# Second convolution over four neighbouring columns at a time, on column tiles of TensorE

## The chip, the cores and the metric

The kernel runs on one core of a Trainium2 chip. The metric is the device time of one execution in microseconds (us). Everything is fp32.

## The reference

The input x has 32 images of 96 channels and 56 x 56 points. Two layers follow each other:

```python
# layer 0
h = depthwise_conv7x7(x) + conv_b                 # per channel
h = layernorm over channels, * ln_g + ln_b
h = gelu(h @ w1 + b1) @ w2 + b2                   # 96 -> 384 -> 96 channels
x = h * layer_scale + x
# layer 1
xs = silu(depthwise_conv5x5(x) + conv_b)          # the "second convolution"
dts, Bs, Cs = split(x_proj_w @ xs)                # 6 + 4 + 4 rows for each point
delta = softplus(dt_w @ dts + dt_b)
log_dA = maximum(delta * A, log(1e-9))            # A < 0, 4 states for each channel
P = exp(cumsum(log_dA)); hs = P * cumsum(delta * Bs * xs / maximum(P, 1e-9))
y = sum over states (hs * Cs) + xs * Ds           # cumsums over the 3136 points
```

## The kernel before

The kernel runs four stages, one behind the other; each hands its result to the next through a buffer in DRAM (`conv1_d`, `block_d`, `conv2_d`), because the axis on partitions changes.

1. *First convolution* (lines 235 to 300). A loop over the 96 channels. Image rows stand on partitions, and a 7x7 depthwise convolution becomes products of TensorE with a banded (Toeplitz) matrix of weights. ScalarE adds the bias (L278), POOL stores to `conv1_d` (L282). Copies of the input into its padded layout are made by POOL (L265), DVE (L262) and ScalarE (L263, L266). The statistics of the layer norm are summed beside it on DVE.
2. *MLP* (lines 306 to 412). A loop over 28 groups of four rows, each for both halves (`s`: even and odd columns) of 448 points. `hidden` multiplies with w1 (L351, row tiles of TensorE), ScalarE applies gelu (L361), `result` multiplies with w2 (L370: four products of 32 output rows each, at four column tiles, one for each of the four image rows). DVE then adds bias and residual (L382), and POOL stores the group's rows of 32 channels to `block_d` (L391), one DMA for each group and block of channels. `normalise` (L341) scales the next group's input on DVE. The order of TensorE and DVE is written out by hand (`pin`): in each step the three parts `hidden`, `result`, `normalise` follow each other for f = 0, 1, 2. Accumulator `po` has two buffers.
3. *Second convolution* (lines 414 to 446). A loop over 96 channels. A tile `xp` holds a channel's 56 rows twice: the even columns on partitions 0 to 55, the odd ones from 64. For each channel three products (taps t = 1, 0, 2) are made for each half of the images (`j`), each with 120 input rows, 128 output rows (56 for even columns, 56 for odd ones, 16 unused) and 432 or 448 points (L429). Two ScalarE passes of 56 rows apply bias and silu and interleave even and odd columns (L441), and POOL stores 56 rows of 7168 bytes to `conv2_d` (L446). SP loads the weights (two DMAs by `toeplitz`, L226) and the two halves of the input (L423) for each channel; `wts` and `xps` have three buffers each, so loads run up to three channels ahead. PSUM has four accumulators.
4. *Scan* (from line 448). A loop over units of 32 channels and 1568 points, with DVE scans (L582, L591), POOL products (L575, L602) and ScalarE exponentials. It reads `conv2_d`.

The tap tables `taps1_d` and `taps2_d` in DRAM are made from the weights in a preparation part at the start (lines 140 to 158), where L153 copies single elements of the 5x5 weights in reversed order.

Of the kernel before, what the change touches and what calls it, by code (L numbers as in the profile page):

```python
# [23 lines left out]
WP = 128  # L24
W2 = W // 2
MP = 64
P1, P2 = (K1 + 1) // 2, (K2 + 1) // 2
CH = 1568
NI = 2
NCH = L // CH  # L30
# [11 lines left out]
def convnext_then_scan_kernel(  # L42
# [25 lines left out]

    conv1_d = dram.tile([C, ROWS, COLS], F32, name="conv1_d")
    block_d = dram.tile([C, ROWS, COLS], F32, name="block_d")
    conv2_d = dram.tile([C, H, B * W], F32, name="conv2_d")
    du_d = dram.tile([B * NCH, C, 2, CH], F32, name="du_d")
    rstd_d = dram.tile([ROWS, COLS], F32, name="rstd_d")
    taps1_d = dram.tile([C, 3 * WP * P1], F32, name="taps1_d")
    taps2_d = dram.tile([C, 3 * WP * P2], F32, name="taps2_d")

    def column(src, n, name):
        t = const.tile([n, 1], F32, name=name)  # L80
# [54 lines left out]
    with tc.tile_pool(name="prep", bufs=1) as prep, tc.tile_pool(  # L135
        name="prep_ps", bufs=1, space=PSUM
    ) as prep_ps:


        for taps_d, cw, k, flip in ((taps1_d, c1w, K1, False), (taps2_d, c2w, K2, True)):  # L140
            kt = prep.tile([C, k, k], F32, name=f"kt{k}")
            nc.sync.dma_start(kt, cw.rearrange("c (i j) -> c i j", j=k))
            pad = prep.tile([C, 3, WP, (k + 1) // 2], F32, name=f"pad{k}")
            nc.vector.memset(pad, 0.0)
            at = H - 1 - k // 2
            for i in range(3):
                for t in range((k + 1) // 2):
                    j = 2 * t + 1 - i
                    if j not in range(k):
                        continue  # L150
                    if flip:
                        for r in range(k):
                            nc.vector.tensor_copy(  # L153
                                pad[:, i, at + r, t : t + 1], kt[:, k - 1 - r, j : j + 1]
                            )
                    else:
                        nc.vector.tensor_copy(pad[:, i, at : at + k, t], kt[:, :, j])
            nc.sync.dma_start(taps_d, pad.rearrange("c d p t -> c (d p t)"))


        cen = prep.tile([C, C], F32, name="cen")
        nc.vector.tensor_scalar(cen, ident[:C, :C], -1.0 / C, None, ALU.add)
        w1g = prep.tile([C, F], F32, name="w1g")
        nc.vector.tensor_scalar(w1g, w1_t, g_t, None, ALU.mult)
        ps = prep_ps.tile([C, 512], F32, name="ps_w1")
        nc.tensor.matmul(ps[:, :F], lhsT=cen, rhs=w1g, start=True, stop=True)
        for i in range(RB):
            for d in range(C // CB):
                nc.vector.tensor_copy(
                    w1r_t[CB * i : CB * i + CB, d, :], ps[CB * d : CB * d + CB, :F]  # L170
                )
        ps = prep_ps.tile([128, 512], F32, name="ps_b1")
        for f in range(3):
            nc.tensor.matmul(
                ps[:, f : f + 1], lhsT=w1_t[:, f * 128 : (f + 1) * 128], rhs=lnb_t,
                start=True, stop=True,
            )
        nc.vector.tensor_add(b1p_t, ps[:, :3], b1_t)

        for f in range(3):  # L180
            nc.vector.tensor_mul(w2_t[:, f, :], w2_t[:, f, :], ls_b)
        b2p_t = prep.tile([C, 1], F32, name="b2p_t")
        nc.vector.tensor_mul(b2p_t, b2_t, ls_t)
        for i in range(RB):
            for d in range(C // CB):
                nc.vector.tensor_copy(
                    b2r_t[CB * i : CB * i + CB, d : d + 1], b2p_t[CB * d : CB * d + CB]
                )

        ps = prep_ps.tile([C, 512], F32, name="ps_wd")  # L190
        nc.tensor.matmul(ps[:, :C], lhsT=xp_t, rhs=dtwT_t, start=True, stop=True)
        nc.vector.tensor_copy(wd_t, ps[:, :C])


        nc.vector.memset(bcw_t, 0.0)
        nc.vector.tensor_copy(bcw_t[:, : 2 * N], xpT_t[:, R:])
        nc.vector.memset(pick_t, 0.0)
        for k in range(4):
            rows = slice(32 * k, 32 * k + 2 * N)
            at = 32 * k + (k // 2) * N  # L200
            nc.vector.tensor_copy(
                pick_t[rows].rearrange("p (d n) -> p d n", n=N),
                ident[rows, at : at + N].rearrange("p (o n) -> p o n", o=1).to_broadcast(
                    [2 * N, DG, N]
                ),
            )
        nc.vector.tensor_reduce(
            sel_t, ident.rearrange("p (d n) -> p d n", n=N), mybir.AxisListType.X, ALU.add
        )
        nc.vector.tensor_scalar(dsm_t, ident[:C, :C], ds_t, None, ALU.mult)  # L210
        nc.scalar.activation(a_t, a_t, AF.Exp)
        nc.vector.tensor_scalar(a_t, a_t, -1.0, None, ALU.mult)
# [19 lines left out]
    def two(t):  # L232
        return t.rearrange("p (s q) -> p s q", s=2)
# [72 lines left out]
    with tc.tile_pool(name="mlp", bufs=2) as pool, tc.tile_pool(  # L306
# [5 lines left out]
        hts: dict = {}  # L312
        xts: dict = {}
        gts: dict = {}
        ots: dict = {}

        def rows_of(d, row, b):
            return d[CB * b : CB * b + CB, row : row + RB, :].rearrange("c r q -> r c q")
# [47 lines left out]
        def result(n, s, d):  # L366
            po = ps_o.tile([128, 512], F32, name=f"po_{n}_{s}_{d}", tag="po")
            for f in range(3):
                for i in range(RB):
                    pin(nc.tensor.matmul(  # L370
                        po[CB * i : CB * i + CB, :HALF],
                        lhsT=w2_t[:, f, CB * d : CB * d + CB],
                        rhs=gts[n, s, f, i // 2][:, i % 2],
                        start=(f == 0),
                        stop=(f == 2),
                        tile_position=(0, CB * i),
                    ))
            if s == 0:
                ots[n, d] = pool.tile([128, COLS], F32, name=f"o_{n}_{d}", tag="o", bufs=5)
            ot = ots[n, d]  # L380
            pairs = "p (i r) -> p i r"
            pin(nc.vector.scalar_tensor_tensor(  # L382
                two(ot)[:, s].rearrange(pairs, i=BI),
                in0=po[:, :HALF].rearrange(pairs, i=BI),
                scalar=b2r_t[:, d : d + 1],
                in1=xts[n, d].rearrange("p (i r s) -> p s i r", i=BI, s=2)[:, s],
                op0=ALU.add,
                op1=ALU.add,
            ))
            if s == 1:  # L390
                nc.gpsimd.dma_start(rows_of(block_d, n * RB, d), ot)  # L391

        groups = ROWS // RB
        parts = groups * 2
# [14 lines left out]
                    normalise(n + 1, f)  # L409


    with tc.tile_pool(name="c2", bufs=3) as pool, tc.tile_pool(
        name="c2k", bufs=1
    ) as keep, tc.tile_pool(name="c2_ps", bufs=4, space=PSUM) as psum:
        wts = [keep.tile([128, 2, MP * P2], F32, name=f"wt2_{i}") for i in range(3)]
        xps = [keep.tile([128, B2, PQ], F32, name=f"xp2_{i}") for i in range(3)]
        for t in wts + xps:
            nc.vector.memset(t, 0.0)
        for c in range(C):
            wv = toeplitz(taps2_d, wts[c % 3], K2, c, MP)  # L420
            xt = xps[c % 3]
            for s in range(2):
                nc.sync.dma_start(xt[MP * s : MP * s + H], by_row(block_d[c], s))  # L423
            ps = psum.tile([128, B2, 512], F32, name=f"ps2_{c}", tag="ps")

            for i, t in enumerate((1, 0, 2)):
                lo, hi = max(0, 1 - t), W2 - max(0, t - 1)
                for j in range(B2):
                    nc.tensor.matmul(  # L429
                        ps[:, j, :PQ].rearrange("p (i r) -> p i r", i=BI)[:, :, lo:hi],  # L430
                        lhsT=wv[:KR, t],
                        rhs=xt[:KR, j].rearrange("p (i r) -> p i r", i=BI)[
                            :, :, lo + t - 1 : hi + t - 1
                        ],
                        start=(i == 0),
                        stop=(i == 2),
                    )
            st = pool.tile([H, B2, BI, W2, 2], F32, name=f"st_{c}", tag="st")
            for s in range(2):
                rows = slice(MP * s, MP * s + H)  # L440
                nc.scalar.activation(  # L441
                    st.rearrange("p j i r s -> p s j i r")[:, s],
                    ps[rows, :, :PQ].rearrange("p j (i r) -> p j i r", i=BI),
                    AF.Silu, bias=c2b_t[rows, c : c + 1], scale=1.0,
                )
            nc.gpsimd.dma_start(conv2_d[c], st.rearrange("p j i r s -> p (j i r s)"))  # L446

# [272 lines left out]
```

## Time and profile before

| | us |
|---|---|
| median of three runs | 3753.94 (3751.75 to 3754.26) |
| the profiled execution | 3750.96 |
| its span, first to last instruction | 3749.2 |
| first convolution, products (L270) | 27 to 608 |
| MLP, products (L351, L370) | 644 to 1487 |
| second convolution, products (L429) | 1506 to 1931 |
| scan | 1945 to the end |

| engine | busy us | share of the span |
|---|---|---|
| TensorE products (PE) | 3181.4 | 85% |
| weight loads (PEld) | 1445.6 | 39% |
| VectorE (DVE) | 2270.6 | 61% |
| ScalarE (ACT) | 2276.7 | 61% |
| GpSimd (POOL) | 1877.6 | 50% |

The profile is of one execution. A line such as L429 is a line of the kernel. A group of instructions is given with its engine, operation, output and input names, the shape (partitions x elements), the count, and behind the bar its busy time, the mean length in ns, and the idle time of the engine ahead of it with what ended that. A window line gives start and end of a stage, its length, the busy time of PE, PEld, DVE, ACT and POOL with their counts, the granted TensorE clock, the DMA share and GB/s. Lengths of matmul records are modelled and overlap, so a mean length times a count is not their busy time.

### The profile page before, as it was taken

What the parts mean: (1) busy time and instruction counts of PE and PEld (TensorE: products, weight loads), DVE (VectorE), ACT (ScalarE), POOL (GpSimd) and SP (SyncE); (2) the same over time, 40 slices, a digit from 0 to 9 for tenths busy, and PEclk for the clock granted to TensorE, in tenths of its full rate; (3) what the DMA queues carried; (4) which work ended last, traced back from release to release, by engine and by line L of the source; (5) the groups of instructions that cost most, each with busy time, mean ns of one, the idle gap of its engine ahead of it and who ended that gap; (6) DMA issues with size and microseconds to landing.
All of it is one profiled execution on the core that took longest, in us unless ns stands there. A gap on an engine that the chain in (4) does not pass through costs nothing. (4 is left out here: it accounts for less than half of the span.)

```text
span 3749.2 us, 41885 instructions
## 1 busy us (share of the span) xinstructions
PE 3181.4 (85%) x15370; PEld 1445.6 (39%) x15370; DVE 2270.6 (61%) x1413; ACT 2276.7 (61%) x2133; POOL 1877.6 (50%) x1085
## 2 busy tenths in 40 slices
PE   7999995999999998999976777877787777777775
PEld 5777773333333333666641222222222222222221
DVE  5666664222222222000008999999999999999998
ACT  3555552433333333444438888788878888888884
POOL 2333331000000000011117889889988988998896
PEclk9999997999999999999986666666767666676766
DMA  5555553455544553777768787778778777777873
GB/s 150 167 168 166 169 165 103 143 160 160 161 157 154 155 157 101 207 220 221 224 178 286 262 272 258 254 278 273 257 260 274 250 261 280 268 259 262 276 253 114
DMA packets 318352, 785.65 MB, mean 210 GB/s; under 512 B 137028, under 2 KB 201860, under 8 KB 293572
## 3 DMA queue, kind: packets, MB, share of 16 engines
q1 hardware_dynamic: 260996, 628.66, 52.2%
q0 software_dynamic: 42816, 115.77, 9.9%
q10 hardware_dynamic: 14336, 38.54, 2.7%
q8 instruction: 122, 2.00, 0.2%
q14 instruction: 82, 0.67, 0.1%
HBM read 550.06 MB, written 232.64 MB: 209 GB/s over the span
## 5 line engine op out<-in xcount | busy, mean ns | idle before, releaser
L602 POOL TENSOR_TENSOR hs<-hs,ct 128x1568 f32<-128x1568 f32 x192 | 672.9, 3505 | 104.1 <-DVE hs L591 89.4
L575 POOL TENSOR_TENSOR rep<-rep,bt 128x1568 f32<-128x1568 f32 x192 | 674.6, 3514 | 14.7 <-DMA rep<-du_d 14.7
L361 ACT ACTIVATE g<-ph,b1p_t 128x896 f32<-128x896 f32 x336 | 320.2, 1004 | 500.7 <-PE ph L351 500.7
L270 PE MATMUL ps<-xq,wt 120*112 120x448 f32 x1536 | 581.8, 540 | 13.0 <-POOL xq L265 13.0
L382 DVE SCALAR_TENSOR_TENSOR o<-po,b2r_t,x 128x448 f32<-128x448 f32 x168 | 114.8, 684 | 636.4 <-PE po L370 620.7
L270 PEld LDWEIGHTS ps<-xq,wt 120*112 120x112 f32 x1536 | 429.4, 280 | 165.0 <-POOL xq L265 13.3
L351 PE MATMUL ph<-h,w1r_t 32*128 32x448 f32 x4032 | 441.2, 561 | 47.8 <-DVE h L341 44.0
L391 POOL DMA_DIRECT2D block_d<-o x84 | 57.9, 689 | 820.2 <-DVE o L382 735.1
L429 PE MATMUL ps<-xp,wt 120*128 120x432 f32 (+1 forms) x1152 | 425.2, 533 | 17.8 <-DMA xp<-block_d 17.8
L506 PE MATMUL pz<-xs,wd_t 96*96 96x392 f32 x512 | 273.5, 699 | 174.1 <-ACT du L514 145.4
L370 PE MATMUL po<-g,w_t 128*32 128x448 f32 x4032 | 413.0, 543 | 0.0
L615 PE MATMUL py<-hs,sel_t 128*32 128x392 f32 x1536 | 332.9, 685 | 79.4 <-POOL hs L602 79.2
L582 DVE TENSOR_TENSOR_SCAN pv<-rep,pv 128x1568 f32<-128x1568 f32 x96 | 329.1, 3428 | 58.3 <-DMA rep<-du_d 41.8
L551 PE MATMUL pk<-bn,pick_t 8*128 8x392 f32 x1024 | 287.1, 678 | 90.5 <-ACT y L625 70.6
L587 DVE SCALAR_TENSOR_TENSOR pv<-pv,rep 128x1568 f32<-128x1568 f32 x192 | 345.6, 1800 | 20.0
L429 PEld LDWEIGHTS ps<-xp,wt 120*128 120x128 f32 x1152 | 289.7, 252 | 153.5 <-issue 21.3
L582 DVE TENSOR_TENSOR_SCAN pv<-rep,carry_p,pv 128x1568 f32<-128x1568 f32 x96 | 334.9, 3489 | 10.0 <-DVE hs L591 0.4
L591 DVE TENSOR_TENSOR_SCAN hs<-rep,carry_h,pv 128x1568 f32<-128x1568 f32 x96 | 334.0, 3480 | 11.1 <-DVE pv L587 1.4
L441 ACT ACTIVATE st<-ps,c2b_t 56x896 f32<-56x896 f32 x192 | 204.4, 1065 | 214.8 <-issue 210.3
L591 DVE TENSOR_TENSOR_SCAN hs<-rep,pv 128x1568 f32<-128x1568 f32 x96 | 328.3, 3420 | 9.9 <-DVE pv L587 0.5
L608 PE MATMUL py<-xs,dsm_t 96*96 96x392 f32 x512 | 314.6, 758 | 13.2 <-ACT bn L539 8.0
L569 ACT ACTIVATE rep<-rep,a_t 128x1568 f32<-128x1568 f32 x192 | 308.3, 1606 | 11.6 <-DMA rep<-du_d 11.3
(84 smaller groups left out, 3335.2 us busy)
## 6 DMA issues: line engine op xcount, KB each, us to landing
rep<-du_d SPq DMA_DIRECT2D x192, 1568.0 KB
du_d<-du SPq DMA_DIRECT2D x128, 588.0 KB
xt<-in_x_dram SPq DMA_DIRECT2D x192, 196.0 KB
h<-conv_d SPq DMA_DIRECT2D x84, 448.0 KB
x<-in_x_dram SPq DMA_DIRECT2D x336, 112.0 KB
block_d<-o POOLq DMA_DIRECT2D x84, 448.0 KB, 11.0
xp<-block_d SPq DMA_DIRECT2D x192, 196.0 KB
conv_d<-st POOLq DMA_DIRECT2D x96, 392.0 KB, 4.5
```

The lines of the kernel that those rows point to most:

```text
L270: nc.tensor.matmul(ps[:, j, :PQ].rearrange("p (i r) -> p i r", i=BI), lhsT=wv[:KR, t], rhs=xq[:KR, j, :, t : t + W2], start=(t == 0), stop ...
L351: pin(nc.tensor.matmul(phs[i // 2][:, i % 2, :HALF], lhsT=w1r_t[rows, d, f * 128 : (f + 1) * 128], rhs=hts[n, d][rows, s * HALF : (s + 1) ...
L361: nc.scalar.activation(gt, ph[:, :, :HALF], AF.Gelu, bias=b1p_t[:, f : f + 1], scale=1.0)
L370: pin(nc.tensor.matmul(po[CB * i : CB * i + CB, :HALF], lhsT=w2_t[:, f, CB * d : CB * d + CB], rhs=gts[n, s, f, i // 2][:, i % 2], start=( ...
L429: nc.tensor.matmul(ps[:, j, :PQ].rearrange("p (i r) -> p i r", i=BI)[:, :, lo:hi], lhsT=wv[:KR, t], rhs=xt[:KR, j].rearrange("p (i r) -> p ...
L575: pin(nc.gpsimd.tensor_mul(ut, ut, bts[i // NG]))
L582: pin(nc.vector.tensor_tensor_scan(run, da, zero, carry_p[:, col : col + 1] if q else 1.0 / EPS, ALU.mult, ALU.add))
L587: pin(nc.vector.scalar_tensor_tensor(run, in0=run, scalar=1.0, in1=ut, op0=ALU.min, op1=ALU.mult))
L591: pin(nc.vector.tensor_tensor_scan(ht, da, run, carry_h[:, col : col + 1] if q else 0.0, ALU.mult, ALU.add))
L602: pin(nc.gpsimd.tensor_mul(ht, ht, cts[k]))
L608: pin(nc.tensor.matmul(half(py[:C], s), lhsT=dsm_t, rhs=tokens(k, 2 * h + s, 4), start=True, stop=False,))
L615: pin(nc.tensor.matmul(py[g * DG : (g + 1) * DG, s, :BK], lhsT=sel_t, rhs=hss[k * NG + g][:, cols], start=False, stop=True, tile_position= ...
```

## The change

The second convolution is laid out anew, and with it what writes its input.

- `block_d` holds, for each channel and row, four sets of 14 columns (`k`), each set with one zero column as padding, in the order in which the second convolution reads it. The two DVE operations of a pair of halves become four, one for each of the four column sets, of 224 elements instead of 448; a group's store becomes four DMAs, one for each image row. Six output buffers are kept and zeroed once.
- The second convolution gives half of the rows (28 of 56) at a time. An input tile holds 30 rows times four column sets, 120 partitions; the tile has 128, and those that aren't loaded stay zero. For each half, two taps and four column sets of the output: eight products of 128 input rows, 32 output rows (28 used) and 448 points, each at its own column tile of TensorE.
- One ScalarE pass over 128 partitions takes the place of two over 56. Its result `yt` has the four column sets on four blocks of 32 partitions, so four copies of 28 rows (one on POOL, three on DVE) interleave the columns into `st`, which POOL stores.
- The weights of a channel come in one DMA of 128 rows of 1 KB from a new tap table.

```diff
-    block_d = dram.tile([C, ROWS, COLS], F32, name="block_d")
+    block_d = dram.tile([C, H, QC, B2, BI * QP], F32, name="block_d")
...
+        turned = prep.tile([C, K2, K2], F32, name="turned")
+        for r in range(K2):
+            nc.vector.tensor_copy(turned[:, r], kt[:, K2 - 1 - r])
+        pad = prep.tile([C, QC, 2 * RW, QC * 2], F32, name="pad2")
+        nc.vector.memset(pad, 0.0)
+        for k in range(QC):
+            for f in range(QC):
+                for t in range(2):
+                    j = 4 * t + (k if k < 2 else k - 4) - f + K2 // 2
+                    if j in range(K2):
+                        nc.vector.tensor_copy(
+                            pad[:, k, RW - K2 : RW, f * 2 + t], turned[:, :, j]
+                        )
+        nc.sync.dma_start(taps2_d, pad)
...
-        ots: dict = {}
+        ots = [
+            pool.tile([128, QC, BI, QP], F32, name=f"o_{i}", bufs=1) for i in range(2 * blocks)
+        ]
+        for t in ots:
+            nc.vector.memset(t, 0.0)
...
-            pin(nc.vector.scalar_tensor_tensor(
-                two(ot)[:, s].rearrange(pairs, i=BI),
-                in0=po[:, :HALF].rearrange(pairs, i=BI),
...
+            for e in range(2):
+                pin(nc.vector.scalar_tensor_tensor(
+                    ot[:, 2 * e + s, :, e : e + QW],
+                    in0=po[:, :HALF].rearrange("p (i a e) -> p e i a", i=BI, e=2)[:, e],
+                    scalar=b2r_t[:, d : d + 1],
+                    in1=xts[n, d].rearrange("p (i a e s) -> p s e i a", i=BI, s=2, e=2)[:, s, e],
...
-                nc.gpsimd.dma_start(rows_of(block_d, n * RB, d), ot)
+                for i in range(RB):
+                    nc.gpsimd.dma_start(
+                        rows[:, i], ot[CB * i : CB * i + CB].rearrange("p k i r -> p k (i r)")
+                    )
...
+            wt = pool.tile([128, RW * QC * 2], F32, name=f"wt2_{c}", tag="wt")
+            taps = taps2_d[c, 0, 0:1, 0:1]
+            step = QC * 2
+            nc.sync.dma_start(
+                wt,
+                bass.AP(
+                    taps.tensor, taps.offset,
+                    [[step, RW], [2 * RW * step, QC], [1, RW * step]],
+                ),
+            )
+            wv = wt.rearrange("p (o f t) -> p f t o", f=QC, t=2)
...
+            for h in range(2):
+                xt = xqs[c % 3][h]
+                rows = block_d[c, (H - RW + 2) * (1 - h) : (H - RW + 2) * (1 - h) + RW - 2]
+                nc.sync.dma_start(
+                    xt[2 * QC * h : 2 * QC * h + (RW - 2) * QC],
+                    rows.rearrange("m k j q -> (m k) (j q)"),
+                )
+                xv = xt.rearrange("p (b r) -> p b r", r=QP)
+                for t in range(2):
+                    for f in range(QC):
+                        nc.tensor.matmul(
+                            ps[RW * f : RW * f + RW, h, : B * QW].rearrange(
+                                "p (b q) -> p b q", q=QW
+                            ),
+                            lhsT=wv[:, f, t],
+                            rhs=xv[:, :, t : t + QW],
+                            start=(t == 0),
+                            stop=(t == 1),
+                            tile_position=(0, RW * f),
+                        )
+            yt = pool.tile([128, 2, B * QW], F32, name=f"yt_{c}", tag="yt")
+            nc.scalar.activation(
+                yt, ps[:, :, : B * QW], AF.Silu, bias=c2b_t[:, c : c + 1], scale=1.0
+            )
+            st = pool.tile([QR, 2, B, QW, QC], F32, name=f"st_{c}", tag="st")
+            for f in range(QC):
+                copy = nc.gpsimd.tensor_copy if f == 0 else nc.vector.tensor_copy
+                copy(
+                    st[:, :, :, :, f],
+                    yt[RW * f : RW * f + QR].rearrange("p h (b q) -> p h b q", q=QW),
+                )
+            nc.gpsimd.dma_start(
+                conv2_d[c].rearrange("(h o) w -> o h w", h=2),
+                st.rearrange("p h b q f -> p h (b q f)"),
+            )
```

## The prediction

> **What bounds the kernel now.** I read the page's slices first, then busy time by stage, then the second convolution's rows, and last the order of time at one group boundary of the MLP.
>
> The stages, with busy time and count of PE, PEld, DVE, ACT and POOL, then granted clock, DMA share and GB/s:
>
> ```profile
> 674.00:1490.00 816.00, 811.29 (x7944) 296.30 (x7940) 195.67 (x249) 312.47 (x328) 57.90 (x84) 1.00 0.48 151
> 1490.00:1506.00 16.00, 0.43 (x1) 0.46 (x2) 3.55 (x6) 0.00 (x0) 0.00 (x0) 0.59 0.50 141
> 1506.00:1930.00 424.00, 424.00 (x1151) 289.08 (x1151) 0.00 (x0) 203.63 (x191) 48.77 (x95) 1.00 0.75 217
> ```
>
> The second convolution (third row) is a TensorE stage: busy for all of its 424 us at full clock, DVE at nothing, POOL issuing DMAs only. But DMA is already at 0.75 there: the second limit stands a quarter away. In the MLP DMA and POOL have room.
>
> Rows by form (busy us, mean ns):
>
> ```profile
> L429 PE MATMUL ps<-xp,wt 120*128 120x432 f32 x768 | 294.7, 527 | 0.0
> L370 PE MATMUL po<-g,w_t 128*32 128x448 f32 x4032 | 413.0, 543 | 0.0
> L441 ACT ACTIVATE st<-ps,c2b_t 56x896 f32<-56x896 f32 x192 | 204.4, 1065 | 214.8 <-issue 210.3 <-PE ps L429 3.2
> L361 ACT ACTIVATE g<-ph,b1p_t 128x896 f32<-128x896 f32 x336 | 320.2, 1004 | 500.7 <-PE ph L351 500.7
> L262 DVE COPY xq<-xt 56x448 f32<-56x448 f32 x96 | 37.5, 390 | 64.1 <-PE ps L270 54.6 <-DMA xt<-in_x_dram 8.9 <-DVE acc L246 0.5
> L265 POOL COPY xq<-xt 56x448 f32<-56x448 f32 x96 | 56.4, 587 | 276.2 <-issue 243.0 <-DMA xt<-in_x_dram 28.6 <-PE ps L270 4.6
> L446 POOL DMA_DIRECT2D conv_d<-st x96 | 49.3, 513 | 395.0 <-ACT st L441 368.3 <-DMA xp<-block_d 26.7
> L391 POOL DMA_DIRECT2D block_d<-o x84 | 57.9, 689 | 820.2 <-DVE o L382 735.1 <-DMA h<-conv_d 78.9 <-issue 6.3
> ```
>
> Each fp32 product shows as two records that overlap, so mean ns is no price; cadence is. L429 runs from 1505.6 to 1930.7 us, 425.1 us for 96 channels: 4.43 us a channel, six products of 0.74 us. L370 is the change's own form, four column tiles of 32 side by side: in the timeline 96 records (12 sets of four products, two records each) take 9.23 us, 0.77 us a set, ends included; start to start it is 0.75 us. A set of four costs what one full product costs.
>
> The MLP's group boundary (start, length):
>
> ```profile
> 1008.37 2.91 PE L351 MATMUL ph<-h,w1r_t 32*128 32x448 f32 x24
> 1008.51 0.68 DVE L382 SCALAR_TENSOR_TENSOR o<-po,b2r_t,x 128x448 f32<-128x448 f32 x1 [3.18 <-PE po L370]
> 1009.11 1.08 DVE L341 TENSOR_TENSOR h<-h,r 128x896 f32<-128x896 f32 x1
> 1010.25 0.31 PEld L351 LDWEIGHTS ph<-h,w1r_t 32*128 32x128 f32 x8 [0.81 <-DVE h L341]
> ```
>
> Elsewhere this L351 group takes 2.54 us; here 2.91, since the third normalise stands behind L382 in DVE's order. So L382 is on the path once a group, 27 times.
>
> **The change part by part.**
>
> *Products.* Six of 0.74 us a channel go; two halves by two taps, four sets of 0.75, come: 3.0 us. The weight loads have 32 columns; L370's four take 0.13 us of every 0.375. With a step of eight words they may take longer: 112 columns at step four take 280 ns (L270), 128 contiguous ones 186 (L351), per column 2.50 against 1.45, x1.72. At twice that, 0.45 us, they would overrun by 0.07 a half set, 0.6 us a channel; at x1.72, 0.22, they hide. I take 3.0.
>
> *ScalarE.* Two L441 of 1.07 become one over 128x896, 1.0 by L361. Beside PE, nothing either way.
>
> *Copies.* New: four of 28x896, output step four words, three on DVE and one on POOL. Lower end for DVE: L262 (input step two) 390 ns for 448; with the 139 ns of a one-element copy (L153) as fixed part that is 0.56 ns an element, so 0.64 us for 896. Upper end: the scans, 3.43 us for 1568, 2.19 ns an element: 2.1 us. Step four is nearest to the weight loads' x1.72, giving 0.139 + 896 x 0.56 x 1.72 = 1.0 us. Three are 3.0, as long as the products. POOL: L265 587 ns, a one-element copy 183 (L601), 0.90 ns an element: 0.99 at the low end, 1.5 with x1.72, 2.1 by the scan stage's POOL product (3505 ns for 1568). Its DMA issue stays 0.51 (56 rows still), and waits for the three DVE copies; queued behind it is only the next channel's POOL copy. 1.5 + 0.5 lies within a period.
>
> *Whether DVE and POOL hinder each other in this* the trace doesn't show: the copies L262 begin 0.07 us after L265 ends, and in the second convolution DVE does nothing. Ends: no cost, or the sum in series, 3 x 1.0 + 1.5 + 0.5 = 5.0 us a channel. The nearest row with both at work is L282, 647 ns for 112 rows beside DVE sums; it lies on one line with L446 (512 for 56) and L391 (688 for 128), so those DVE operations delay no DMA issue. I take no cost, and keep 5.0.
>
> *A rule against this change:* the Trainium skill, "SBUF — State Buffer", section "SBUF: two separate sides", says that VectorE in a two-port mode and GpSimd lock each other out of a shared port pair for whole instructions, DMA issues included; no run here shows it yet. By it the copies would cost the series sum and the kernel would be slower. The same skill, "Vector Engine (DVE) Microarchitecture Reference", section 5.2, has ports lose speed whenever single words hop; L262 with step two shows no loss at 0.56 ns an element, so that rule is too strict for step two, and step four is open.
>
> *Transfers.* A channel now loads 2 x 112 rows of 1792 B and 2 x 112 of 768 B, and stores 56 rows of 7168 B. After: 240 rows of 1920 B, 128 of 1 KB, the same store: about 970 KB for 952. The stage's queue shares (q1 48.3%, q0 26.0% of 16 engines) are 34.5 and 18.6 engine-us a channel. MLP loads cost 0.172 us per 3.5 KB packet; with the second convolution's 432 data packets and 567 KB this solves to 0.025 us a packet plus 0.042 a KB, so 33.4 for the new loads. 33.4 + 18.6 = 52 engine-us, over 16 engines 3.25 us at a share of 1.00. The best slices of this kernel are at 0.9 or more (319 GB/s at the scan's start), so 0.93: 3.5 us. Loads run two channels ahead (three buffers), as now.
>
> So a channel is the longest of PE 3.0, DVE 3.0 to 3.1, DMA 3.5: **3.5 us**, 336 for 96, and 425.1 - 336 = **89 us saved**. What is late next is DMA, not TensorE.
>
> *MLP.* L382 becomes two of 224 elements. L382 costs 684 = 448 x 1.04 + 217; its successor starts 0.60 after it. Two plain ones are 2 x 0.45, start to start 2 x 0.37, +0.14 us; with the x1.72 on the stepped operands 2 x 0.60, +0.44. Times 27 boundaries: 4 to 12 us, I take **+8**; in the other places DVE's idle time (3.2 us before each) hides it. Below nothing is excluded: no work goes. One block_d store of 128 rows becomes four of 128: 0.69 to 2.76 us of POOL, 336 issues, 232 us in an 816 us stage where POOL is 7% busy. At the end they show: three tiles come 2.26 us apart and need 2.76 each, so the last issue starts near 1492.1 for 1488.8; but each moves 120 KB, and conv1_d's 196 KB land in 3.8 us where block_d's 448 take 11. Landing near 1496 for 1498.8: **-3**. If they land as slowly as now, +3. The zeroing of six buffers (5 us) lies in DVE's 18 us before the first normalise.
>
> *Rest.* The tail from the last product to its store is one ScalarE pass and three copies for two passes, 1.0 + 3.0 for 2.1: **+2**. Preparation has ten small copies fewer, a longer zeroing, and 768 KB written for 432 ahead of the first loads: **+1** (0 to 2).
>
> Sum: -89 + 8 - 3 + 2 + 1 = -81. The profiled execution took 3750.96 us (span 3749.2, 1.8 around it); it would take 3670. The median of the runs is 3.0 above it, so I forecast **3673**.
>
> **Rivals.**
> 1. *Series.* POOL's copy and issue wait for DVE's copies and the reverse. For: a DVE copy at over one element per 1.04 ns (L262) is something DVE's two-input operations here never reach, so it may take what POOL also needs. Against: nothing measured. With DVE 1.0, POOL copy 1.3 to 1.5, issue 0.5: 4.85 us, 466 in all, +41, and with the other terms (+8) **3802**, slower. It decides from a series sum over 4.35 us: with DVE copies of 0.64 and POOL's 0.99 it is only 3.4 and the forecast stands.
> 2. *Copies alone, partly hindered, or DVE at 1.3 us each:* about 4.0 us, 384 in all, -41 + 8: **3721**.
> 3. *TensorE still bound:* DMA delivers 970 KB in 3.0 us. Against: 52 engine-us in 48. 290 in all, -135 + 8: **3627**.
> 4. *It gives nothing:* a sum near 4.35, within 0.2%.
>
> **How the numbers follow.** About 0.2% is what a measurement of this kernel can tell from no change. Forecast case (3.3 to 3.7 us a channel, 3654 to 3693): 0.42. TensorE: 0.08. Partly hindered: 0.20. Nothing: 0.03. Series: 0.27. So faster 0.70, same 0.03, slower 0.27. The range runs from 3635 (3.1 us a channel) to 3815 (5.0, the series end); outside lie most of the TensorE case and the worst series, some 0.15. Both signs hold much, so the likeliest's own range, 3654 to 3693, stands beside it.
>
> **What would show it.** Right: PE in the second convolution idle before its products, released by the load of xq, DMA at 0.9 or above, matmul sets of 0.75 us, DVE copies at or under 1.05. Wrong by rival 1: DVE or POOL copies far longer than 1.5 us, or starting only as the other ends, PE released by ScalarE or by its banks, DMA share below 0.75. Rival 3: PE busy throughout at 3.0. In the MLP L351's boundary group at 3.0 to 3.4 for 2.91; if it stays, +8 is wrong.

## The result, and the profile after

The changed kernel takes 3782.97 us (median of four, 3781.73 to 3784.25) for 3752.85 us before: 1.008 times as long, 95% interval 1.0063 to 1.0098. It is slower by 30 us where 3673 was forecast; it went the way of the first rival, the series, which stood at 3802.

The second convolution by stage (start and end, length, busy time and count of PE, PEld, DVE, ACT and POOL, granted clock, DMA share, GB/s), after:

```profile
1512.00:1940.00 428.00, 310.93 (x3072) 115.60 (x3064) 415.09 (x271) 94.95 (x94) 305.81 (x181) 0.99 0.78 215
```

TensorE's work fell as forecast, from 424 us to 311, but DVE, which did nothing in this stage, is now busy for 415 of 428 us. The bound has moved to DVE, and DMA at 0.78 is not at its limit.

The groups, by form:

```profile
L489 DVE COPY st<-yt 28x896 f32<-28x896 f32 x288 | 437.3, 1518 | 16.3 <-ACT yt L483 10.8
L472 PE MATMUL ps<-xq,wt 128*32 128x448 f32 x3072 | 311.3, 549 | 126.3 <-ACT yt L483 114.1 <-DMA xq<-block_d 11.6 <-DMA wt<-taps_d 0.6
L489 POOL COPY st<-yt 28x896 f32<-28x896 f32 x96 | 246.0, 2635 | 16.6 <-DMA wt<-taps_d 16.0 <-DMA conv_d<-st 0.5
```

DVE's copies have a mean of 1518 ns, and POOL's 2635, for 1.0 and 1.5 us assumed. TensorE waits for ScalarE, and ScalarE in turn for DVE, in the list of waits (total, times, longest):

```profile
ACT yt L483 <- DVE st L489: 329.9, 91, 4.3
```

A mean hides what matters here. The same line by its shortest, median and longest record:

```profile
L489 DVE COPY st<-yt x288: 939/1035/2966, 1519.7 to 1962.3; 28x896 f32<-28x896 f32 x144
L489 POOL COPY st<-yt x96: 1997/2622/3183, 1519.7 to 1961.5; 28x896 f32<-28x896 f32 x96
```

The median DVE copy is 1.03 us, as assumed. 95 of the 288 take about 2.5 us and raise the mean. Where these stand is seen in the order of time (start, length), DVE first, then POOL:

```profile
1704.09 2.60 DVE L489 COPY st<-yt 28x896 f32<-28x896 f32 x1
...
1706.72 2.54 DVE L489 COPY st<-yt 28x896 f32<-28x896 f32 x1
...
1709.28 2.04 DVE L489 COPY st<-yt 28x896 f32<-28x896 f32 x2
```

```profile
1703.26 5.12 POOL L489 COPY st<-yt 28x896 f32<-28x896 f32 x2
1708.22 1.16 POOL L493 DMA_DIRECT2D conv_d<-st  x1
1711.92 0.59 POOL L493 DMA_DIRECT2D conv_d<-st  x1 [2.54 <-DVE st L489]
```

Two POOL copies, 5.12 us, lie beside two long DVE copies, 2.60 and 2.54; the two DVE copies at 1709.28, with no POOL copy beside them, take 2.04 together. Each long copy is 1.0 us plus some 1.55 us, and each POOL copy of 2.6 is one DVE copy of 1.0 plus 1.6. This fits two engines that take turns and record the waiting as length; the experiments below test it. From store to store a channel takes (1965.3 - 1525.0) / 95 = 4.63 us, which is 3 x 1.03 + 1.54. The store's issue has no place in this sum.

Where the profile's 33.2 us of longer span went, from the starts in the two traces: MLP +12.2 (its last group of w2 products starts at 1490.8 for 1478.5), hand-over to the second convolution -6.2 (first product at 1511.6 for 1505.6), second convolution from first product to last store +25.9 (453.6 for 427.7), store to first scan product +0.5, scan +0.7.

The MLP's group boundary after (TensorE, then DVE):

```profile
1013.42 1.79 PE L371 MATMUL ph<-h,w1r_t 32*128 32x448 f32 x16
1015.76 1.03 PE L371 MATMUL ph<-h,w1r_t 32*128 32x448 f32 x8 [0.55 <-DVE h L361]
```

```profile
1013.56 1.14 DVE L401 SCALAR_TENSOR_TENSOR o<-po,b2r_t,x 128x224 f32<-128x224 f32 x2 [2.72 <-PE po L390]
1014.61 1.09 DVE L361 TENSOR_TENSOR h<-h,r 128x896 f32<-128x896 f32 x1
```

The pair of DVE sums takes 1.05 us from start to start where one sum took 0.60, and the normalise behind it comes that much later: the L371 group takes 3.30 us from its start to that of the next products, for 2.85 before.

### The profile page after: what moved, and what is told of

Its sections match the earlier page's. It is cut to its first block, busy times and chain, and to the rows that moved or that the text cites. A ratio compares the mean times of both kernels' runs of the same rounds, so it can differ in the third digit from the quotient of the medians.

```text
span 3782.4 us, 46657 instructions
## 1 busy us (share of the span) xinstructions
PE 3068.1 (81%) x17290; PEld 1274.2 (34%) x17290; DVE 2788.7 (74%) x1865; ACT 2169.2 (57%) x2037; POOL 2275.0 (60%) x1433
## 5 line engine op out<-in xcount | busy, mean ns | idle before, releaser
L401 DVE SCALAR_TENSOR_TENSOR o<-po,b2r_t,x 128x224 f32<-128x224 f32 x336 | 190.6, 609 | 572.7 <-PE po L390 572.7
L413 POOL DMA_DIRECT2D block_d<-o x336 | 183.1, 552 | 709.0 <-DVE o L401 621.9
L371 PE MATMUL ph<-h,w1r_t 32*128 32x448 f32 x4032 | 440.9, 560 | 60.2 <-DVE h L361 58.9
L489 DVE COPY st<-yt 28x896 f32<-28x896 f32 x288 | 437.3, 1518 | 16.3 <-ACT yt L483 10.8
L472 PE MATMUL ps<-xq,wt 128*32 128x448 f32 x3072 | 311.3, 549 | 126.3 <-ACT yt L483 114.1
L658 PE MATMUL py<-xs,dsm_t 96*96 96x392 f32 x512 | 304.9, 738 | 9.8 <-ACT ct L605 4.5
L620 ACT ACTIVATE rep<-rep,lift_t 128x1568 f32<-128x1568 f32 x192 | 307.6, 1602 | 6.3
```

What stands on the lines that cost most here:

```text
L371: pin(nc.tensor.matmul(phs[i // 2][:, i % 2, :HALF], lhsT=w1r_t[rows, d, f * 128 : (f + 1) * 128], rhs=hts[n, d][rows, s * HALF : (s + 1) ...
L472: nc.tensor.matmul(ps[RW * f : RW * f + RW, h, : B * QW].rearrange("p (b q) -> p b q", q=QW), lhsT=wv[:, f, t], rhs=xv[:, :, t : t + QW], ...
L489: copy(st[:, :, :, :, f], yt[RW * f : RW * f + QR].rearrange("p h (b q) -> p h b q", q=QW),)
```

## The experiments

Double rate here means DVE's copy mode: without an output step it took 0.53 ns an element (0.618 us for 896, less 139 ns for a copy of one element), where two-input sums took 1.04 ((1092 - 157) / 896, L287 of the kernel before). The theory, after the result: while DVE copies at double rate, a POOL copy can't run, and the reverse, so the four copies of a channel stand in series. Rivals: DVE's copies are slow by themselves, by their step of four words and their change of partitions; the loads set the period; any DVE instruction excludes POOL, not only the copies at double rate. The periods below are store to store, as above. Each ratio is to the kernel before as measured along with that run (3750 to 3751 us, where it was 3752.85 beside the changed kernel), so absolute times of different runs compare to a few us only.

**One copy off POOL.**

```diff
-                copy = nc.gpsimd.tensor_copy if f == 0 else nc.vector.tensor_copy
+                copy = nc.scalar.copy if f == 0 else nc.vector.tensor_copy
```

> The copy of column set 0 goes from POOL to ScalarE; POOL only issues the store. Series theory (a DVE copy of 1.0 us and a POOL copy of 1.6 us don't run at once, so a channel takes 3 x 1.0 + 1.6 = 4.6 us): DVE copies all fall to about 1.04, a channel takes 3.1 (DVE) to 3.5 us (DMA), 3638 to 3676 us. Rival, DVE copies slow by themselves (mean 1.52 us by step and partition shift): DVE unchanged, 4.6 us a channel, about 3780. Rival, loads set the period: about 3780 too, with DVE now idle between copies.

Measured: 3662.88 us, 0.9765 of before (0.9749 to 0.9781): 120 us under the changed kernel. A channel takes 3.41 us. The DVE line alone, in this kernel:

```profile
L489 DVE COPY st<-yt x288: 939/1037/1493, 1521.0 to 1848.7; 28x896 f32<-28x896 f32 x144
```

The same three copies a channel, nothing changed in them, and the 2.5 us records are gone; 51 of the 288 still take 1.1 to 1.5 us, and with less loaded (below) none is over 1.09. So they weren't slow by themselves, and the loads did not set the period of 4.63 us. Without the hindrance the kernel comes to about 10 us from the forecast of 3673.

**All four on DVE.**

```diff
-                copy = nc.gpsimd.tensor_copy if f == 0 else nc.vector.tensor_copy
+                copy = nc.vector.tensor_copy
```

> All four copies on DVE. Series theory: 4 x 1.04 = 4.15 us a channel for 4.62, 45 us less, about 3738. DVE copies slow by themselves: 4 x 1.52 = 6.1 us, 142 us more, about 3925. Loads set the period: no change, 3783.

Measured: 3734.41 us, 0.9957 of before (0.9942 to 0.9972); a channel takes 4.13 us, the copies 1.01 on the mean. A fourth copy added to DVE, which the profile shows as the bound, makes the kernel 49 us faster (46 by the ratios), since it takes POOL's away.

**Two on ScalarE, two on DVE.** The same line with `nc.scalar.copy if f < 2`.

> Column sets 0 and 1 on ScalarE, 2 and 3 on DVE. Series theory: DVE 2.1 us, ScalarE 1.0 + 2 x 1.0 = 3.0, TensorE 3.0, DMA 3.25 at a share of 1.00: 3.1 to 3.5 us a channel, 3638 to 3676. If that is the same as with one copy on ScalarE, DVE isn't what is left there, and DMA share at 0.9 or more says it is DMA; if it is under 3.1 it was DVE. DVE copies slow by themselves: 2 x 1.52 = 3.0, also 3640 to 3680 but with DVE copies of 1.5 us.

Measured: 3790.28 us, 1.0107 of before. A miss of the expectation: a ScalarE copy with this output step takes 1.89 us, not 1.0, so ScalarE's pass and two copies are 1.0 + 2 x 1.89 = 4.8 us; a channel takes 4.73 and ScalarE is busy for 297 of 300 us. On the theory it says little (DVE's copies are 1.0 with no POOL copy beside them, as in the two runs before), and it shows that one copy was as much as ScalarE could take without becoming the bound.

**Copies without the step.**

```diff
-            st = pool.tile([QR, 2, B, QW, QC], F32, name=f"st_{c}", tag="st")
+            st = pool.tile([QR, 2, QC, B, QW], F32, name=f"st_{c}", tag="st")
...
-                    st[:, :, :, :, f],
+                    st[:, :, f],
```

> The four copies write with step one instead of four words: the columns of a row are left in sets, not interleaved, in what the scan reads. Engines as in the changed kernel. Series theory: DVE 0.64 and POOL about 1.0 us, 3 x 0.64 + 1.0 = 2.9 us in series, below TensorE's 3.0 and DMA's 3.25 to 3.5: 3635 to 3676; some DVE copies still show POOL's length on top. Loads set the period: no change, 3783. It prices the step itself: DVE 1.0 against 0.64, POOL 1.6 against 1.0.

Measured: 3659.19 us, 0.9757 of before; 3.36 us a channel. DVE's median copy is 0.618 us for 1.035, POOL's shortest 0.92. The longest DVE copy is 1.27, and POOL's median 1.31, so both still carry some of the other's time, but the series sum of 3 x 0.62 + 0.9 fits below the transfers, as the second of the next two windows shows.

**Which limit comes next.** In the kernel with one copy on ScalarE, and in this last one, 1540 to 1800 us of each (columns as above):

```profile
1540.00:1800.00 260.00, 247.82 (x2524) 97.32 (x2516) 247.01 (x231) 221.24 (x152) 49.81 (x76) 1.00 0.98 300
```

```profile
1540.00:1800.00 260.00, 244.91 (x2524) 110.44 (x2520) 169.20 (x228) 77.70 (x77) 151.29 (x152) 1.00 0.98 298
```

DMA share 0.98 in both, with quite different loads on DVE, ScalarE and POOL. To tell it apart, less is loaded:

```diff
-            nc.sync.dma_start(
-                wt,
...
+            if c == 0:
+                nc.sync.dma_start(
+                    wt,
```

> As a1_act_copy, but the weights of channel 0 are loaded once and serve all channels (the other channels' own weights are left out): 128 KB of 970 less for each channel. That kernel took 3.44 us a channel with DMA at 0.97. DMA theory: the period falls to DVE's 3 x 1.04 = 3.1 to 3.2 us, 23 to 32 us less, 3631 to 3640, DMA at about 0.9. If the 3.44 was DVE or ScalarE: no change, 3663.

Measured: 3647.30 us, 15.6 less than with all weights; 3.24 us a channel, DMA at 0.91, DVE busy for 251 of 260 us. So the transfers set the 3.41 us, as the forecast had it, but the gain is smaller than expected. DVE, with 3 x 1.04 = 3.12 us of the 3.24, is most likely what comes next.

**DVE at single rate.** The three DVE copies read a second operand from PSUM.

```diff
-                copy(
-                    st[:, :, :, :, f],
...
+                    nc.vector.scalar_tensor_tensor(
+                        st.rearrange("p h b q f -> p f (h b q)")[:, f],
+                        in0=yt[RW * f : RW * f + QR].rearrange("p h x -> p (h x)"),
+                        scalar=1.0,
+                        in1=nil[:QR, :1].to_broadcast([QR, 2 * B * QW]),
+                        op0=ALU.mult,
+                        op1=ALU.add,
+                    )
```

> The three DVE copies become two-input sums with a zero in PSUM (one SBUF input, no double rate); POOL keeps its copy; three accumulators for four. If DVE's double-rate copy is what excludes POOL: the DVE operations take 1.1 us (step free) to 1.7 us (step x1.72) and POOL's copy runs beside them at its own length of about 1.6 us; no DVE operation is 2.5 us long; a channel takes 3.4 (DMA) to 5.2 us, 3660 to 3830, by that length alone. If any DVE operation excludes POOL: one DVE operation in three still carries POOL's 1.6 us on top, a channel takes 4.9 to 6.7 us, 3810 to 3980.

Measured: 3861.98 us, 1.030 of before; 5.45 us a channel. The two lines in this kernel:

```profile
L496 DVE SCALAR_TENSOR_TENSOR st<-yt,nil x288: 1710/1788/1929, 1518.9 to 2040.8; 28x896 f32<-28x896 f32 x144
L491 POOL COPY st<-yt x96: 1760/1880/1982, 1518.9 to 2034.9; 28x896 f32<-28x896 f32 x96
```

This is the clearest of the runs. All DVE operations are alike (1.71 to 1.93 us) and so are all POOL copies (1.76 to 1.98); the period is three DVE operations, 3 x 1.79 = 5.4 us, and POOL's 1.88 lie beside them. With DVE at single rate, and busy all of the time, nobody waits for the other, though both still read and write the same tiles as in the changed kernel. So not every DVE operation excludes POOL, and sharing tiles is not the reason. The run changes the rate, the operation and the second operand together. That the rate is what counts is supported by the scan, in a trace that was there before the forecast: two-input DVE operations with both inputs in SBUF run there at (1800 - 157) / 1568 = 1.05 ns an element, almost always with a POOL product beside them, and all 192 take 1799 to 1800 ns, the POOL products 3482 to 3539. In the kernel before:

```profile
L587 DVE SCALAR_TENSOR_TENSOR pv<-pv,rep 128x1568 f32<-128x1568 f32 x192 | 345.6, 1800 | 20.0
L602 POOL TENSOR_TENSOR hs<-hs,ct 128x1568 f32<-128x1568 f32 x192 | 672.9, 3505 | 104.1 <-DVE hs L591 89.4 <-ACT rep L571 4.2 <-ACT ct L555 1.1
```

A DVE copy at single rate beside POOL was not run, so that the double rate alone is the reason is the best reading, not shown by itself. This kernel is slower because at single rate the stepped output costs DVE (1788 - 157) / 896 = 1.82 ns an element, with the 157 ns of a one-element copy (L636 of the changed kernel) as fixed part.

**Two on POOL.** `nc.gpsimd.tensor_copy if f < 2`.

> Column sets 0 and 1 copied by POOL, 2 and 3 by DVE. Series theory: 2 x 1.0 + 2 x 1.6 = 5.2 us a channel for 4.62, about 56 us more than the changed kernel, 3839, though no engine's own work comes to more than 2 x 1.9 + 0.6 = 4.4 us. If the two engines ran side by side: POOL alone, 2 x 1.9 + 0.6 = 4.4 us, about 3762.

Measured: 3860.31 us, 1.0293 of before; 5.45 us a channel. Side by side it would have been near before; the series theory has the direction and 5.2 of 5.45 us. The rest is not seen as a wait: in the order of time a channel is a POOL copy with no DVE copy ahead of it (1.84 us), 0.88 us from its end to the end of the DVE copy that waited, 1.0 for the next DVE copy, and 1.63 from there to the end of the second POOL copy, 5.4 in all. The store's issue lies beside these; its median is 1.14 us here, and 0.59 in the single-rate kernel, and 89 of the 96 issues end 0.11 us after a DVE copy has ended. POOL's issue waits for DVE's copies as well.

**The MLP's order.** In the hand-written order `normalise` is put ahead of `result`:

```diff
+                if k % 2 and n + 1 < groups:
+                    normalise(n + 1, f)
                 if k:
                     result((k - 1) // 2, (k - 1) % 2, f)
-                if k % 2 and n + 1 < groups:
-                    normalise(n + 1, f)
```

> The changed kernel with normalise ahead of result in the hand-written order of the MLP, so that the two DVE sums of a step no longer stand ahead of the next group's third normalise. At a group boundary TensorE's L371 group took 3.30 us from start to start for 2.47 elsewhere. Theory (DVE's order costs 0.83 us at each of 27 boundaries): 22 us less, 3761, and no wait of TensorE for h at the boundaries. Rival (the loads of h end that wait): no change, 3783.

Measured: 3758.74 us, 24 less than the changed kernel, and 1.0021 of before (1.0011 to 1.0031). All L371 groups but the stage's first are 2.54 us long.

> The kernel before with normalise ahead of result. Its boundary group took 2.85 us from start to start for 2.47: 27 x 0.38 = 10 us less, about 3741, if DVE's order is the cause there too; no change, 3751, if the loads of h are.

Measured: 3740.07 us, 0.9971 of before (0.9960 to 0.9982), 10 less. Each taken against the kernel before as measured along with it, the changed kernel stands at +30.1 us, and at +7.6 with normalise first: 22.5 less. That is 12 more than the 10 here, and it fits the +12.2 that the trace gives to the second DVE sum.

**Both together.** One copy on ScalarE and `normalise` first.

> The copy of set 0 on ScalarE as in a1_act_copy, and normalise ahead of result. If both act on their own stage: 3663 - 22 = 3641. If the boundary's wait is of loads: 3663.

Measured: 3640.35 us, 0.9706 of before (0.9691 to 0.9720). The two act on their own stages and add up; this is the fastest of all.

## Why the prediction failed

*Products and ScalarE.* Right. Four column tiles at 0.75 us a set, start to start (the 311 us of busy time hold the modelled ends); one pass of 1.007 us.

*Copies.* DVE's length was right: 1.0 us taken, and 1.02 measured where nothing hinders it. That has some luck in it: the factor of 1.72 came from TensorE's weight loads, and the runs give (1.02 - 0.14) / (0.62 - 0.14) = 1.8 for DVE's copy. POOL's copy was mis-sized: 1.88 us by itself, for 1.5; only its part in the series, 1.54, is near.

*"Whether DVE and POOL hinder each other ... I take no cost, and keep 5.0."* This is the step that failed. The runs show 4.63 us a channel, near the end in series, against 3.41 with POOL's copy given to ScalarE. The row I took as nearest, the store issues L282 beside DVE's sums, was the wrong row: those sums run at 1.04 ns an element, the single rate. The copies run at 0.53 without the step, and with it at 1.0 where the single-rate operation takes 1.82; DVE left POOL alone only in the slower mode. The scan's rows (L587 and L602 above) have DVE and POOL side by side too, but also at single rate, so they would have misled in the same way; no row of DVE at the copies' rate beside POOL stood in that trace. The rival named just this as its ground "for"; its weight should have gone ahead of a row of another mode. Its price of 4.85 us was too high by 0.2: the store's issue, priced at 0.5, lies beside the copies (alternately 0.59 and 1.16 us), and POOL's copy counts 1.54 for 1.35. That is 96 x 0.22 = 21 us too much; the other terms came to about +13 us in the profile (33.2 less 96 x 4.63 - 425.1) for the +8 taken, so that 3802 lies as near to 3783 as it does is partly chance.

The rule of the Trainium skill that stood against the change ("SBUF — State Buffer", section "SBUF: two separate sides") agrees with these runs: DVE at double rate and POOL excluded each other for almost whole instructions (2.6 us for 1.0; of POOL's 1.88 us all but some 0.3 stand in the series), and DVE at single rate with one SBUF input did not (1.79 and 1.88 side by side). Of the second, "Vector Engine (DVE) Microarchitecture Reference", section 5.2, the part left open is now measured: at step four DVE loses, 1.82 ns an element for 1.04 at single rate, while at step two (L262) it lost next to nothing, 0.56 for the 0.53 of a copy without step.

*Transfers.* Right, and shown only once POOL's copy was gone: 3.41 us a channel at a share of 0.98, for 3.5 forecast with 0.93. The sum behind it took 432 packets and 567 KB where its own row counts give 448 and 560; with these it gives 33.3 for 33.4.

*MLP.* The mechanism was right, +12.2 us for +8 taken out of 4 to 12: the stepped operands cost the upper end, 0.61 us for each sum of 224. *Hand-over.* -6.2 for -3: an issue took POOL 0.55 us, not 0.69, and the smaller stores land in 5.7 us for 11; what each gave was not separated.

*Rest.* The tail can't be told apart from the series of copies that ends the stage. Of preparation's +1, the first convolution's first product starts 0.8 us later and its last 0.2 later.

## What to carry to other kernels

Two engines that stand idle don't run side by side for that alone when work is moved to them: where DVE copies SBUF to SBUF at double rate, give POOL nothing to copy in that stage, or give up the double rate; here a fourth DVE copy cost less than POOL's help. When a trace lacks two operations side by side, take as nearest a row with the same rate, not the same engine. And read shortest, median and longest of a group before its mean: two lengths in one form may be a wait inside the instruction.

## What the runs showed of the hardware

An output step of four words lengthened the copies: DVE's at double rate 1.02 us for 0.62, POOL's 1.88 us for 0.92 (its shortest). DVE at single rate took 1.82 ns an element with the step, and 1.04 in the sums without it. ScalarE's stepped copy took 1.89 us, for 1.007 of its pass over 896 elements with step one; that pass reads PSUM and the copy SBUF, so this doesn't show the step alone. I had counted on ScalarE's at 1.0. The wait of DVE and POOL for each other is recorded as part of an instruction's length, on both engines, so that the bound engine looked busy for 97% of the stage while a third of that was waiting. The store's issue on POOL stretched from 0.59 us to as much as 1.15 beside DVE's copies, with its end 0.11 us behind the end of a copy. Two-input DVE operations on SBUF and POOL products in the scan did not lengthen each other (1799 to 1800 and 3482 to 3539 ns). DMA held a share of 0.98 and 300 GB/s for 260 us with loads of 1 to 2 KB runs.
